# Image-wise window attention inside the merged plan, and layer 3 experts in three groups, in a four-layer kernel on one Trainium2 core

## The chip, the cores and the metric

The kernel runs on one core of one Trainium2 chip. The metric is device time in microseconds of one execution. A core has five engines with queues of their own, which wait for each other through semaphores: PE (matrix products into PSUM), DVE (vector work), ACT (activation functions), POOL (here it mostly issues indirect DMAs) and SP (issues plain DMAs). Each engine takes its instructions strictly in the order in which they were written into its queue.

## The reference, cut to what matters

The input is two images of 256 channels and 32 x 32 positions, all in fp32. Four layers follow each other. Layers 0 and 1 are attention over image positions and are not touched. Then the images become tokens `t` (two images of 1024 tokens of width 256), and layers 2 and 3 follow:

```
t = t + window_attention(layernorm(t))      # layer 2: 8 heads of 32, windows of 64 tokens, relative bias, shifted by 32
t = t + experts2(layernorm(t))              # 8 experts, hidden 1024, each token goes to its best 2, weights renormalised
t = t + additive_attention(layernorm(t))    # layer 3: e[i,j] = Wa . tanh(q[i] + k[j] + bh), softmax over the 1024 keys
t = t + experts3(layernorm(t))              # 8 experts, hidden 512, each token goes to its best 2
x = tokens back to channels
```

The window attention's softmax runs inside a window of 64 tokens, so an image's result depends on that image alone, as do the additive attention and the experts. In the last window of an image some pairs are masked.

## The kernel before, in words

Tokens lie in `t`, 16 tiles of 128 (8 for each image). Up to and with layer 1 a scheduler of the framework, or an order written out in `attention` and `shared_attention`, sets the instructions' order; both kernels have the same instructions there. After that come two parts.

*Window attention* (`window_attention`, L682 to 808). All 16 tiles are normalised (`layer_norm`, L89), turned to channels (`to_channels`, L103), and then treated tile by tile in one function with pools of its own: `project` makes queries and keys for four tiles at once (products L727, evictions of 32 partitions x 512 by turns on ACT L735 and DVE L737), `scores` makes values and scores (L747, L759), the scale and bias (L764), maximum and subtraction (L768, L769) and the exps (L772), and `values` turns the weights (L777), copies them (L779 on ACT, L780 on DVE), multiplies (L783), divides, turns, and applies the output matrix (L796). POOL adds the result to `t` (L801). Products use a PSUM pool of two buffers, the scores one of two, the turned weights one of their own, the values two. The framework's scheduler orders all of it. When the last tile of image 0 is through, `after` puts the whole of image 0's `dispatch` for layer 2 into the stream, so it runs beside the window attention of image 1.

*The merged plan* (`Late.run`, L1391). Everything else is a list of generators. Each generator's body stops at `yield` after a piece of work. The list gives each a start, an end and a number of pieces on a scale of its own; a heap takes the generator that is due next, lets it issue one piece, and puts it back by (end - start) / pieces. This writes out a fixed order for every engine (`manual_schedule`); no piece moves by itself at run time, and a piece whose inputs are late holds up what stands behind it on the same engine.

The generators, for layer `l` and image `b`:

- `dispatch(l, b)`: normalises 8 tiles in two halves (`normed`), finds each token's two experts and its slot (`route`, some 60 small DVE operations, products L1023 and L1055), in layer 2 normalises again, and writes the tokens into `slots_in[b]` in DRAM by 16 indirect DMAs on POOL (L989), two for each tile. Last it adds the second bias (L998 to L1004).
- `experts(l, b)`: 23 slot tiles of 128 slots (16 full ones and 7 for the experts' remainders). For each: two indirect DMAs on POOL fetch the expert's weights (L1140, three buffers each), SP loads the slots (L1150), PE turns them (L1158), up products (L1183), bias on DVE (L1188), gelu on ACT (L1172), down products (L1197), a copy on DVE (L1201), and SP stores the tile to `slots_out[b]`.
- `collect(l, b)`: 16 indirect gathers on POOL (L1241, eight buffers), weighted sums into `t` (L1254); in layer 2 then the norm and the projections for the additive attention (`project`, L1294), in layer 3 the way back to channels (`finish`, L1271) and the output.
- `additive(b)`: 64 steps, each four tanhs of 128 x 1024 on ACT (L1322, eight buffers) and eight products with a narrow picking matrix (L1331); after some of the tiles a batch of softmax exps (L1349), and then a turn (L1361) and a values product (L1368) for each tile, one a step.

PSUM of the plan: `misc`, two buffers for all small products, one for `ps_x`, two for `ps_h`, one for `ps_y`, and two banks for `ps_e` of the additive attention.

The order of the plan is: experts of layer 2, image 0, with image 1's dispatch; collect 0 and the start of image 1's experts; these with additive attention of image 0; collect 1; additive attention of image 1 with dispatch, experts and collect of layer 3 of image 0; and then dispatch, experts and collect of layer 3 of image 1, with nothing beside them.

## Time and profile before

| what | us |
|---|---|
| median of three runs (lowest, highest) | 3222.25 (3217.42, 3225.37) |
| the profiled execution's own time | 3233.88 |
| its span, first to last instruction | 3232.2 |
| PE busy (share of the span) | 2927.0 (91%) |
| DVE busy | 1886.4 (58%) |
| ACT busy | 2000.8 (62%) |
| POOL busy | 390.9 (12%) |

One execution is profiled; its time is given beside its span, since sums over the profile are sums over that execution. A PE that counts as busy isn't always at its peak: products overlap, and their ends are modelled. The profile counts an fp32 product with 128 or more columns as two records. A line of the kernel can be that of a helper that many parts call, so groups are told apart by the tiles they write. "Idle before" tells what ended the wait of an engine; it costs something only where that engine is what the end waits for. The last instruction of layer 1 is at about 1790 us in the span; the window attention ends at 2022, and the plan takes the rest.

### The profile page before, as it was taken

How to read it: one execution, taken by the hardware profiler on the slowest of the kernel's cores; microseconds unless marked ns; L12 is line 12 of the kernel's file. 1: busy time of each engine (PE TensorE's matmuls, PEld its weight loads, DVE VectorE, ACT ScalarE, POOL GpSimd, SP SyncE). 2: the span in 40 equal slices, each digit the busy share in tenths (PEclk: the TensorE clock that was granted, in tenths of full speed). 3: DMA queues.
4: the chain of work that ended last, by engine and by line, in shares of the span. 5: the costliest groups of instructions: out<-in, count | busy, mean ns of one | idle time of the engine just before them, and what ended most of it. 6: DMA issues, size and time to landing. Idle time of an engine off the chain costs nothing. (4 is left out here: it accounts for less than half of the span.)

```text
span 3232.2 us, 71102 instructions
## 1 busy us (share of the span) xinstructions
PE 2927.0 (91%) x29260; PEld 1890.0 (58%) x29260; DVE 1886.4 (58%) x3668; ACT 2000.8 (62%) x2990; POOL 390.9 (12%) x544
## 2 busy tenths in 40 slices
PE   7999999999999998999999788888699988999565
PEld 4566666666666665566676565776566633564355
DVE  5998898989898986354454574532422243222423
ACT  1887887878788875565566231111399878979200
POOL 3000000000000000000000002232311011322043
PEclk9999999999999998999999887899799998999688
DMA  3000000000000001000000100765554310543066
GB/s 119 3 3 3 3 3 3 3 3 3 3 3 3 3 3 28 1 1 1 1 2 2 24 1 27 269 232 205 208 182 172 134 30 19 175 147 95 19 229 198
DMA packets 175859, 206.85 MB, mean 64 GB/s; under 512 B 118368, under 2 KB 144880, under 8 KB 163760
## 3 DMA queue, kind: packets, MB, share of 16 engines
q0 software_dynamic: 34848, 167.82, 14.8%
q1 hardware_dynamic: 139248, 34.04, 4.8%
q8 instruction: 230, 3.77, 0.5%
q14 instruction: 93, 0.76, 0.1%
q10 hardware_dynamic: 1440, 0.47, 0.1%
HBM read 172.97 MB, written 28.57 MB: 62 GB/s over the span
## 5 line engine op out<-in xcount | busy, mean ns | idle before, releaser
L314 ACT ACTIVATE sc<-sc,sa_shift 128x1024 f32<-128x1024 f32 x512 | 585.1, 1148 | 53.5 <-DMA sa_shift<-sa_min 53.4
L1322 ACT ACTIVATE th<-kT,qb 128x1024 f32<-128x1024 f32 x512 | 541.0, 1134 | 73.7 <-PE ps_e L1331 58.3
L277 PE MATMUL ps_s<-kT,qT 64*32 64x512 f32 x8192 | 504.4, 596 | 9.0 <-ACT sc L287 8.7
L353 PE MATMUL ps_o<-wt,v 128*64 128x128 f32 x6144 | 503.4, 276 | 0.0
L353 PEld LDWEIGHTS ps_o<-wt,v 128*64 128x64 f32 x6144 | 442.2, 137 | 42.6 <-issue 42.6
L327 DVE STREAM_TRANSPOSE wt<-sc 128x768 f32<-128x768 f32 x512 | 465.7, 943 | 1.0 <-ACT sc L314 1.0
L287 ACT COPY sc<-ps_s 128x1024 f32<-128x1024 f32 x256 | 257.4, 1006 | 115.9 <-PE ps_s L277 42.7
L1172 ACT ACTIVATE h<-hb 128x512 f32<-128x512 f32 x138 | 86.1, 624 | 388.0 <-DVE hb L1188 333.8
L1183 PEld LDWEIGHTS ps_h<-xe,ew 128*128 128x128 f32 x2208 | 275.3, 201 | 79.3 <-issue 56.6
L1183 PE MATMUL ps_h<-xe,ew 128*128 128x128 f32 x2208 | 289.9, 288 | 30.4 <-DMA ew<-in_l_up,rt_rows 28.0
L298 DVE TENSOR_REDUCE sa_least<-sc 128x1 f32<-128x1024 f32 x256 | 306.1, 1196 | 1.9 <-ACT sc L287 1.9
L284 DVE TENSOR_SCALAR_CACHE_REDUCE sc<-ps_s 128x1024 f32<-128x1024 f32 x256 | 301.3, 1177 | 5.9 <-PE ps_s L277 5.9
L1331 PE MATMUL ps_e<-th,pick 128*32 128x512 f32 x2048 | 295.2, 616 | 1.4 <-DVE sc_a L1338 1.4
L1197 PE MATMUL ps_y<-ew,h 128*128 128x256 f32 x1104 | 260.6, 386 | 3.9 <-ACT h L1172 2.7
L1188 DVE TENSOR_TENSOR hb<-ps_h,ew 128x512 f32<-128x512 f32 x138 | 95.3, 691 | 280.8 <-PE ps_h L1183 239.2
L154 DVE TENSOR_SCALAR_CACHE_REDUCE sc<-ps_s 128x1024 f32<-128x1024 f32 x128 | 151.8, 1223 | 179.3 <-PE ps_s L148 179.3
L353 PE MATMUL ps_o<-wl,v_odd 128*64 128x128 f32 x2048 | 252.1, 277 | 0.0
L277 PEld LDWEIGHTS ps_s<-kT,qT 64*32 64x32 f32 x8192 | 126.9, 106 | 200.8 <-issue 171.4
L1197 PEld LDWEIGHTS ps_y<-ew,h 128*128 128x128 f32 x1104 | 204.5, 192 | 59.8 <-issue 20.5
L335 PEld LDWEIGHTS ps_t<-ident,sc 128*128 128x128 f32 x1024 | 107.5, 141 | 216.1 <-issue 169.1
L353 PEld LDWEIGHTS ps_o<-wl,v_odd 128*64 128x64 f32 x2048 | 221.3, 137 | 0.0
L335 PE MATMUL ps_t<-ident,sc 128*128 128x128 f32 x1024 | 168.5, 287 | 4.8 <-ACT wl L336 4.1
(269 smaller groups left out, 3607.1 us busy)
## 6 DMA issues: line engine op xcount, KB each, us to landing
xr<-slots_in SPq DMA_DIRECT2D x92, 128.0 KB
slots_out<-y SPq DMA_DIRECT2D x92, 128.0 KB
sa_got<-sa_least SPq DMA_DIRECT2D x512, 0.5 KB
sa_shift<-sa_min SPq DMA_DIRECT2D x512, 0.2 KB
slots_in<-zero POOLq DMA_DIRECT2D x46, 128.0 KB
sa_sums<-sa_total SPq DMA_DIRECT2D x256, 1.0 KB
xT<-in_x SPq DMA_DIRECT2D x4, 496.0 KB
sb_l_w_in<-in_l_w_in SPq DMA_DIRECT2D x1, 1536.0 KB
```

The costliest lines, as they stand in the source:

```text
L277: nc.tensor.matmul(ps[r][S * c : S * (c + 1), a, :].rearrange("p (b i) -> p b i", i=S), lhsT=qT[half, p, S * i : S * (i + 1)], rhs=keys[ha ...
L284: nc.vector.tensor_scalar(scores[m][0], flat[0], 1.0, None, ALU.mult, ALU.min, accum_out=least[m // 2][:, 0, h : h + 1])
L287: nc.scalar.copy(scores[m][1], flat[1])
L298: nc.vector.tensor_reduce(least[m // 2][:, 1, h : h + 1], scores[m][1], AX.X, ALU.min)
L314: nc.scalar.activation(scores[m][r], scores[m][r], AF.Exp, bias=shift[m // 2][:, r : r + 1], scale=-1.0, accum_out=total[i][:, 2 * p + r, ...
L327: nc.vector.transpose(weights[i, h][:, 2 * p + r, :], scores[m][r][:, :DIRECT])
L335: nc.tensor.transpose(ps[:, g, r, :], s[:, at : at + P], self.ident)
L353: nc.tensor.matmul(sums[i][64 * k : 64 * (k + 1)], lhsT=values, rhs=w, start=(h == 0 and j == 0 and t == 0), stop=(h == 1 and j == 1 and t ...
L1183: nc.tensor.matmul(ps[:, j, :], lhsT=a[:, c, at : at + P], rhs=x[:, c, :], start=(c == 0), stop=(c == CC - 1),)
L1197: nc.tensor.matmul(ps, lhsT=h[:, j, :], rhs=w2[:, j, :], start=(j == 0), stop=(j == HB - 1))
L1322: nc.scalar.activation(h, keys, AF.Tanh, bias=self.qb[b][:, s // G, g : g + 1])
L1331: nc.tensor.matmul(pe[i][c * U : (c + 1) * U, a, :], lhsT=self.pick[:, k, :], rhs=h[:, a, :], start=(k == 0), stop=(k == G - 1),)
```

## The change

- The norm over all tiles, its way to channels and `window_attention` go. `windows(b)` does one image as a generator of the plan, with 128 columns a projection instead of 512, and a fixed order: in step `i` the scores and weights of tile `i`, the turn of tile `i - 1`, the projection of `i + 1`, the back-turn of `i - 2`, the values of `i - 1` and the output of `i - 3`. All its products but scores and values use the plan's two `misc` buffers.
- The plan has names, and each entry tells which others must have been issued before it. Image 0's windows are alone at the start (W0); then come image 0's dispatch (D20) and experts (E20) with image 1's windows (W1) and its dispatch (D21).
- Layer 3's experts are in three groups: image 0 (16 slot tiles and 7), and the two halves of image 1 (8 and 7, that is 15 slot tiles each). The first half's dispatch may start when the additive attention has issued half of image 1; its experts lie beside the second half. The second half alone comes after it.
- Pools: window and additive parts share SBUF and PSUM in phases (`open`); the gather has five buffers and runs two tiles ahead (eight and four before); the additive scores have three buffers (four); softmax batches end after tiles 3, 6, 8 for image 0 and 2, 4, 6, 7, 8 for image 1 (before: 4, 7, 8 for both).

```diff
+GROUPS = {
+    (2, 0): range(0, IT), (2, 1): range(IT, NT),
+    (3, 0): range(0, IT), (3, 1): range(IT, IT + IT // 2), (3, 2): range(IT + IT // 2, NT),
+}
+SLOT_TILES = {IT: 2 * N // TILE + E - 1, IT // 2: N // TILE + E - 1}
...
-            late = Late(ctx, self, t)
-            with tc.tile_pool(name="tok2", bufs=1) as tok2:
...
-                self.window_attention(t, u, uT, after)
-            late.run()
+            Late(ctx, self, t).run()
...
-    def dispatch(self, l, b):
+    def dispatch(self, *key):
...
-        for half in range(2):
-            yield from self.normed(b, half)
-        yield from self.route(l, b)
+        for half in range(n // 4):
+            yield from self.normed(key, tokens, half)
+        yield from self.route(key, n)
...
-                y = self.sb.tile([P, C], F32, name="got", bufs=8)
+                y = self.moe.tile([P, C], F32, name="got", bufs=5)
...
-        for i in range(4):
+        for i in range(2):
             gather(i)
-        yield
+            yield
...
+    def windows(self, b):
+        nc, t, H, D = self.nc, self.t, 8, 32
+        tokens, key = GROUPS[2, b], ("w", b)
+        for half in range(2):
+            yield from self.normed(key, tokens, half)
...
+        def project(g):
+            q[g] = sb.tile([D, H, P], F32, name="qh")
+            k[g] = sb.tile([D, H, P], F32, name="kh")
+            for o in range(2 * CC):
+                ps = self.misc([P, P], "ps_qk")
+                for c in range(CC):
+                    nc.tensor.matmul(
+                        ps, lhsT=self.w_qkv[:, c, o * P : (o + 1) * P], rhs=uT[:, c, g * P : (g + 1) * P],
+                        start=(c == 0), stop=(c == CC - 1),
+                    )
+                for r in range(4):
+                    to = (q if o < CC else k)[g][:, (o % CC) * 4 + r, :]
+                    rows = slice(D * r, D * (r + 1))
+                    if r % 2:
+                        nc.scalar.activation(to, ps[rows, :], AF.Identity, bias=self.b_qk[rows, o : o + 1])
+                    else:
+                        nc.vector.tensor_scalar(to, ps[rows, :], self.b_qk[rows, o : o + 1], None, ALU.add)
+                yield
...
+        yield from project(0)
+        for i in range(IT + 3):
+            if i < IT:
+                scores(i)
+                weigh(i)
+            yield
+            if 0 < i <= IT:
+                turn(i - 1)
+            yield
+            if i + 1 < IT:
+                yield from project(i + 1)
+            if 1 < i <= IT + 1:
+                back(i - 2)
+            yield
+            if 0 < i <= IT:
+                values(i - 1)
+            if 2 < i:
+                output(i - 3)
+            yield
...
-        batches = {3: range(4), 6: range(4, 7), 7: range(7, 8)}
+        ends = (3, 6, 8) if b == 0 else (2, 4, 6, 7, 8)
+        batches = {e - 1: range(d, e) for d, e in zip((0, *ends), ends)}
...
-            (self.experts(2, 0), 0, 185, 72),
-            (self.dispatch(2, 1), 5, 165, 48),
-            (self.collect(2, 0), 186, 225, 18),
-            (self.experts(2, 1), 186, 480, 72),
-            (self.additive(0), 226, 535, 65),
-            (self.collect(2, 1), 482, 525, 18),
-            (self.additive(1), 536, 850, 65),
-            (self.dispatch(3, 0), 546, 622, 40),
-            (self.experts(3, 0), 625, 790, 50),
-            (self.collect(3, 0), 795, 840, 11),
-            (self.dispatch(3, 1), 880, 900, 40),
-            (self.experts(3, 1), 905, 1000, 50),
-            (self.collect(3, 1), 1001, 1040, 11),
+            "W0": (self.windows(0), (), -110, 0, 74),
+            "W1": (self.windows(1), ("W0",), 1, 175, 74),
+            "D20": (self.dispatch(2, 0), ("W0",), 1, 60, 48),
+            "E20": (self.experts(2, 0), ("D20",), 62, 280, 72),
+            "D21": (self.dispatch(2, 1), ("W1",), 176, 272, 48),
+            "C20": (self.collect(2, 0), ("E20", "W1"), 281, 325, 20),
+            "E21": (self.experts(2, 1), ("D21",), 281, 600, 72),
+            "A0": (self.additive(0), ("C20",), 326, 640, 65),
+            "C21": (self.collect(2, 1), ("E21",), 601, 642, 20),
+            "A1": (self.additive(1), ("C21", "A0"), 643, 960, 65),
+            "D30": (self.dispatch(3, 0), ("A0",), 655, 710, 36),
+            "E30": (self.experts(3, 0), ("D30",), 715, 850, 50),
+            "C30": (self.collect(3, 0), ("E30",), 855, 890, 13),
+            "D31": (self.dispatch(3, 1), ("A1 half",), 830, 870, 24),
+            "E31": (self.experts(3, 1), ("D31",), 880, 965, 34),
+            "C31": (self.collect(3, 1), ("E31",), 1030, 1050, 8),
+            "D32": (self.dispatch(3, 2), ("A1",), 970, 1000, 24),
+            "E32": (self.experts(3, 2), ("D32",), 1001, 1060, 34),
+            "C32": (self.collect(3, 2), ("E32",), 1061, 1080, 8),
```

## The prediction

> **What bounds the kernel now.** I read the slices of the page first (the TensorE clock falls and PE has gaps only after 1790 us), then the busy time by stage. I cut the stages at the starts and ends of lines L1183 (up), L1322 (tanh) and L1241 (gather) in the timeline.
>
> ```profile
> 1815.00:2022.00 207.00, 171.32 (x1193) 127.52 (x1191) 120.51 (x333) 58.06 (x98) 29.50 (x45) 0.79 0.03 11
> 2029.00:2259.00 230.00, 197.34 (x1222) 176.54 (x1222) 92.29 (x278) 33.11 (x50) 55.00 (x57) 0.93 0.65 237
> 2278.00:2595.00 317.00, 305.29 (x2094) 204.74 (x2097) 91.50 (x212) 252.74 (x267) 46.67 (x50) 0.97 0.47 170
> 2595.00:2672.00 77.00, 59.59 (x313) 24.36 (x312) 34.13 (x99) 53.83 (x54) 15.32 (x16) 0.91 0.10 29
> 2672.00:3004.00 332.00, 312.51 (x1900) 163.24 (x1904) 97.13 (x264) 294.49 (x300) 74.75 (x78) 0.94 0.33 107
> 3004.00:3100.00 96.00, 34.23 (x116) 21.67 (x109) 33.35 (x135) 2.78 (x4) 21.34 (x22) 0.57 0.14 47
> 3100.00:3199.00 99.00, 90.27 (x594) 81.42 (x592) 33.38 (x67) 14.49 (x23) 37.87 (x40) 0.99 0.84 283
> 3199.00:3232.20 33.20, 5.58 (x17) 2.95 (x16) 10.74 (x21) 0.00 (x0) 15.30 (x16) 0.58 0.34 99
> ```
>
> Columns: stretch, length, busy PE, weight loads, DVE, ACT, POOL (us), clock, DMA share, GB/s. The rows are: window attention of both images, with image 0's dispatch in its middle; layer 2 experts of image 0; experts of image 1 beside additive attention of image 0; the collect between; additive attention of image 1 beside layer 3 experts of image 0; then, with nothing beside it, image 1's layer 3 dispatch, experts and collect. Rows 3 and 5 have little idle PE. The last three, 228 us, run alone; the sixth is a latency chain. Its cause stands in the chain of waits: each scatter waits for the one before.
>
> ```profile
> 3068.78 2.40 DMA slots_in<-u,rt_slot
> 3071.45 2.41 DMA slots_in<-u,rt_slot
> 3074.12 2.42 DMA slots_in<-u,rt_slot
> ```
>
> They start 2.67 us apart; 16 take 42.7 us, and the experts' weight fetches stand behind them on POOL.
>
> The third view is the timeline of ACT and DVE in the window attention:
>
> ```profile
> 1858.65 0.68 ACT L735 ACTIVATE qh<-ps_mm,sb_b_qk 32x512 f32<-32x512 f32 x1 [4.30 <-DVE qh L737]
> 1860.14 1.45 ACT L735 ACTIVATE qh<-ps_mm,sb_b_qk 32x512 f32<-32x512 f32 x2 [0.81 <-DVE qh L737]
> 1859.36 1.52 DVE L737 TENSOR_SCALAR qh<-ps_mm,sb_b_qk 32x512 f32<-32x512 f32 x2 [0.75 <-ACT qh L735]
> ```
>
> The four evictions of one product go by turns: while one engine reads that PSUM tile the other waits.
>
> [...]
>
> **The change, part by part** (against the profiled execution: span 3232.2, own time 3233.9, which is 11.6 over the median of 3222.25). I set new times of the same events against the old ones.
>
> *Image 0's attention alone.* Norms and the first evictions come at 1816 (1815 now; the query weights still load first). Then one tile after another, in the order written. From its scores: DVE scale, max, subtract 3 x 0.69 = 2.1; ACT two exps 1.3 and a copy of turned weights 0.6, by 4.1. All products share two PSUM buffers, so the next tile's projection starts only when that copy frees one: product and hand-over 0.7, then sixteen evictions of 32x128. They are not in the trace; 32x512 takes 0.74 and 0.68, [...] 0.35 is my value (0.27 to 0.40, from a 128x128 ACT copy at 0.27 and a DVE step of that size at 0.40). By turns, three slots a product, they end 5.1 later at 9.8. Transposes, values, output, v and scores then go over PE and the freed buffers, 3 to 3.5. A tile takes 13 us (11 to 14). First tiles 1816 to 1842.5, five at 13, drain 17.5: 1925. (Now: some 43 us for four tiles, 10.7 each, ordered by the scheduler.)
>
> *Image 0's dispatch, with image 1's attention begun.* DVE does both: 59 us of listed operations (four half norms at 7.4, from 4 x (0.40 + 0.18 + 0.41) + 12 x 0.165 + 2 x 0.69; the second norm 8, routing 14, two softmax tiles and projections 7), 6 for gaps of 0.03 between 190 small ones, 9 waiting for PE transposes, router and turns. The first scatter comes at 2000. Fifteen more steps of 2.67 give 2040; image 0's weight fetches are queued behind them, at 2042; fetch to first up product was 6.5 (2022.4 to 2028.9): 2048, against 2029 now. Now the scatters (1943 to 1995) hide behind image 1's attention; in the new order only two and a half of its tiles are there to cover them. Cost 19.
>
> *Image 0's experts with the rest of image 1's attention.* A dense tile is 7.2 us (y copies, L1201, at 2233.15, 2240.39, 2247.64) and that is PE. A window tile is 7.4 us of PE: 32 records at 0.11, 8 at 0.216, 32 score records at 0.03, ten transposes at 0.11. Some 7 of 8 are left, 51 us, over 14 expert tiles: 14 x 7.2 + 51/0.95 + 0.8 a tile for in-order waits and table loads = 166. On POOL every window tile puts a memset and an add (0.7 to 1.0) between weight fetches, and the add waits for DVE; I cost that at nothing, because fetches run two to three tiles, over 20 us, ahead. Without that cover it would be about 1 us for each of eight tiles. Nine tiles are left, 65, with image 1's dispatch, 10, and late fetches, 10: 85. The end is 2299 against 2259: +40. (Now the scatters stretch six tiles to 10 to 16 us each; that loss of 37 goes, since the scatters stand behind nearly all fetches. It is in the 85.)
>
> *Collect 0.* Twelve gathers stand ahead of image 1's first fetch, where it was eight or nine: +4 at 0.96 each. Experts begin at 2322, +44. The stretch up to image 1's first tanh keeps its 394 us: three more tanh steps lie beside the experts (+6) and three fewer beside the collect.
>
> *Additive attention of image 1.* It has 64 steps of four tanhs. Layer 3 experts of image 0 stand after step 12 in the new order (19 in the old). Their dispatch, which begins with the stage, takes 34 us to its first scatter (as 3016 to 3049.5 now), 43 of scatters and 8 to the first product: +85, some 15 us after PE comes to them. PE waits in order, and ACT, two steps of buffers ahead, soon after. Then 28 steps x 1.72 + 23 tiles x 3.73 + 4 values jobs x 4.3 = 151 of PE, /0.96 = 157 (now 172 for 37 steps). Six steps at 4.6 and the dispatch's products: 34. Then the added fifteen tiles: 56, with 16.5 steps 28 and three jobs 13, /0.96 = 101; 8 for their scatters behind collect's gathers. Together 385 (365 to 405) against 332: +53. Splitting the last image makes 30 tiles of 23, and the first 15 are paid here, since PE was already 312 of 332 busy.
>
> *Tail.* Now 228. The half group needs one norm half less and smaller routing: first scatter at +36 (45.5 now), eight scatters 21.4, +8 to the first product: +65. Fifteen tiles at 4.25 and the second group's collect beside them, eight gathers on POOL and four more stores on SP among the loads: 70 (99 now). Four token tiles to collect: 23 (33 now). 158: -70.
>
> Sum: 44 + 53 - 70 = +27; 3222.25 + 27 is about **3249**. Two more exp batches in image 1 cost 2 x 2 x 1.28 = 5 on ACT, behind PE there. Smaller gather buffers cost nothing while three us pass from issue to use (five buffers at 0.96). Bounds: the front 44 (15 to 75), additive stage 53 (30 to 75), tail -70 (-62 to -80).
>
> **Rivals.** *Faster, the added tiles are free.* The place is the additive stage of image 1: were its PE records long only because PE waits inside, fifteen tiles would ride on ACT's 294 of 332 us. For it: the clock is 0.94 and the tanhs pace that stage. Against it: experts beside it run 6 to 12 us a tile where alone they take 4.2. Growth 10 instead of 53: 27 - 43 = -16, 3206; it decides once the growth is under 16. With the front at its low bound of 15 as well, 3177. *Same:* window tiles at the present 10.7 (eight save 18) and the dispatch 10 quicker: 27 - 28, 3221. *Slower still:* window products in image 0's experts stop PE at the two shared buffers: 2 us in each of 14 tiles, 28, and a second dispatch late by 17: 27 + 45, 3294.
>
> **How the numbers follow.** About 0.3% (10 us) is what a measurement of this kernel can tell from none. Main case, slower by 10 to 50: 0.50; slower still: 0.13; the same: 0.13; faster: 0.24. Range 3188 to 3300; the main case alone 3232 to 3272.
>
> **What would show it.** Right: image 0's first up product at 2035 to 2060; scores of image 0 some 13 us apart; image 1's tanhs over 370 us; 155 us from the last tanh to the end. Wrong: tanhs of image 1 within 345 us, or the first experts ending before 2265; either gives the faster case.

## The result and the profile after

The changed kernel takes 3353.07 us (median of four; 3350.96 to 3362.24) beside 3223.4 for the kernel before on the same chip: ratio 1.0411, 95% interval 1.0387 to 1.0435. On another chip it took 3354.4 beside 3241.3: 1.0357 (1.0335 to 1.0379). So it is slower by 113 to 130; the kernel before differs more from chip to chip than the changed one. The profiled executions have spans of 3349.7 and 3232.2 us, 117.5 apart, and all stage times below are theirs.

| event, us in the span | before | forecast | changed |
|---|---|---|---|
| image 0's windows added to `t`, last tile | 1912.7 | 1925 | 1950.5 |
| first scatter, layer 2 image 0 | 1943.1 | 2000 | 2014.5 |
| first up product, image 0 | 2028.9 | 2048 | 2077.2 |
| last expert tile, image 0 | 2259.3 | 2299 | 2332.6 |
| first up product, image 1 | 2278.0 | 2322 | 2373.8 |
| first tanh of image 1 | 2672.3 | 2716 | 2754.3 |
| last tanh | 3003.7 | 3101 | 3186.6 |
| end of the span | 3232.2 | 3259 | 3349.7 |

Up to image 1's first tanh the loss is 82 (44 forecast), in its additive stage 101 (53), and behind it there is a gain of 65 (70). The busy time by stage of the changed kernel, with the columns of the prediction's first fence:

```profile
1810.80:1950.50 139.70, 118.53 (x651) 96.80 (x649) 55.85 (x131) 40.66 (x96) 6.09 (x14) 0.57 0.00 1
1950.50:2077.20 126.70, 60.45 (x276) 43.68 (x276) 70.09 (x263) 11.99 (x30) 21.69 (x26) 0.52 0.16 60
2077.20:2332.60 255.40, 231.76 (x1680) 214.41 (x1678) 130.60 (x363) 74.64 (x127) 55.08 (x64) 0.95 0.55 198
2332.60:2373.80 41.20, 15.52 (x41) 7.56 (x42) 16.80 (x54) 0.00 (x0) 22.60 (x23) 0.59 0.48 163
2373.80:2754.30 380.50, 358.55 (x2386) 224.62 (x2385) 115.90 (x278) 308.83 (x323) 57.12 (x60) 0.96 0.39 139
2754.30:2848.00 93.70, 73.79 (x315) 27.39 (x313) 35.17 (x137) 58.98 (x57) 21.27 (x22) 0.75 0.15 53
2848.00:3020.30 172.30, 163.51 (x1130) 112.71 (x1130) 54.65 (x140) 134.96 (x142) 37.75 (x40) 0.97 0.49 159
3020.30:3077.40 57.10, 35.54 (x176) 11.40 (x169) 19.22 (x67) 35.25 (x34) 29.36 (x30) 0.64 0.37 117
3077.40:3186.60 109.20, 104.30 (x722) 70.84 (x720) 30.47 (x65) 85.18 (x90) 22.65 (x24) 0.98 0.49 160
3186.60:3349.70 163.10, 89.13 (x483) 73.19 (x480) 54.15 (x162) 13.40 (x20) 51.56 (x54) 0.75 0.44 147
```

In order: image 0's windows alone; its dispatch; its experts; the collect; experts of image 1 with additive attention of image 0; then image 1's additive stage in four pieces (ahead of, during and behind image 0's layer 3 experts, and with the half group's); the tail. In the first row PE is busy for 118.5 of 139.7 us, and yet its clock is 0.57. In row 4 POOL and DMA work while PE waits. Rows 6 and 8 are stretches of the additive stage in which both PE and ACT have idle time.

The timeline of PE in one tile of image 0's windows shows what the first row is made of (start, duration in us, engine, line, operation, count):

```profile
1870.19 0.69 PE L1237 MATMUL ps_o<-ident,o 128*128 128x128 f32 x2 [0.29 <-ACT kh L1176]
1870.67 3.46 PE L1226 MATMUL ps_av<-va,w_ptT 128*128 128x33 f32 x16
1873.94 2.05 PE L1245 MATMUL ps_wo<-sb_wa_w_out,oT 128*128 128x256 f32 x4
1875.79 1.91 PE L1186 MATMUL ps_va<-sb_w_qkv,uT 128*128 128x256 f32 x4
1877.63 1.97 PE L1198 MATMUL ps_s<-kh,qh 32*64 32x64 f32 x32
```

There is no gap between these; the sixteen values records take 0.22 us each. (They are eight products: in these traces an fp32 product of 33, 64 or 8 columns counts as two records too, and only a turn as one.) In the kernel before, where the clock went up and down within the window stage (0.79 on average), eight such records took 1.05 us in a stretch at clock 1.00 (1848.7 to 1849.8), where eight take 1.73 here at 0.50:

```profile
1848.71 1.05 PE L783 MATMUL ps_av<-va,ptT 128*128 128x33 f32 x8 [0.53 <-ACT ptT L779]
```

The changed kernel's steady tiles are 17.3 us apart (the scaled scores, L1205, at 1897.1, 1914.4 and 1931.6), where 13 were forecast. PE's waits over four such tiles, 1862 to 1932 (us in total, how many, the longest):

```profile
PE ps_qk L1168 <- DVE w_ptT L1221: 5.5, 4, 1.8
PE ps_qk L1168 <- ACT qh L1176: 1.2, 4, 0.3
PE ps_o L1237 <- ACT kh L1176: 1.2, 4, 0.3
```

That is 8 us in 70: PE is hardly kept waiting, it is slow. The next three fences are lines of POOL's timeline: at the end of image 0's layer 2 experts in the changed kernel, the first gather at that place in the kernel before, and ahead of the first half group's experts in the changed kernel (gathers between the lines shown are left out):

```profile
2343.58 0.97 POOL L827 DMA_INDIRECT slots_in<-u,rt_slot  x1 [1.70 <-DMA slots_in<-u,rt_slot]
2344.85 0.98 POOL L1082 DMA_INDIRECT got<-slots_out,rt_slot  x1 [0.30 <-issue]
```

```profile
2261.94 0.96 POOL L1241 DMA_INDIRECT got<-slots_out,rt_slot  x1 [20.37 <-issue]
```

```profile
3056.13 1.08 POOL L1082 DMA_INDIRECT got<-slots_out,rt_slot  x1 [1.02 <-DVE t L1095]
3064.01 1.08 POOL L1082 DMA_INDIRECT got<-slots_out,rt_slot  x1 [5.54 <-DVE t L1095]
3067.96 0.95 POOL L979 DMA_INDIRECT ew<-in_l_up,rt_rows  x1 [0.30 <-issue]
```

Image 0's last expert tile was out at 2332.6, but its gathers stand behind image 1's late scatters until 2344.9, 12.3 us later; in the kernel before it was 2.6 (2259.3 to 2261.9). And the half group's first weight fetch stands behind image 0's sixteen gathers, which themselves wait for the sums that free their five buffers.

### The profile page after: what moved, and what is told of

Its sections match the earlier page's. It is cut to its first block, busy times and chain, and to the rows that moved or that the text cites. A ratio compares the mean times of both kernels' runs of the same rounds, so it can differ in the third digit from the quotient of the medians.

```text
span 3349.7 us, 72263 instructions
## 1 busy us (share of the span) xinstructions
PE 2994.4 (89%) x29638; PEld 1966.7 (59%) x29638; DVE 1947.5 (58%) x3892; ACT 2051.0 (61%) x3107; POOL 402.5 (12%) x558
## 5 line engine op out<-in xcount | busy, mean ns | idle before, releaser
L1022 PEld LDWEIGHTS ps_h<-xe,ew 128*128 128x128 f32 x2320 | 282.2, 197 | 61.5 <-issue 42.4
L1022 PE MATMUL ps_h<-xe,ew 128*128 128x128 f32 x2320 | 297.0, 283 | 11.6 <-DMA ew<-in_l_up,rt_rows 4.7
L1036 PE MATMUL ps_y<-ew,h 128*128 128x256 f32 x1160 | 277.7, 389 | 15.8 <-DMA ew<-in_l_down,rt_rows 9.2
L1324 PE MATMUL ps_e<-th,pick 128*32 128x512 f32 x2048 | 283.7, 633 | 5.4 <-DVE sc_a L1331 5.4
L1036 PEld LDWEIGHTS ps_y<-ew,h 128*128 128x128 f32 x1160 | 217.1, 194 | 81.6 <-issue 33.5
L1040 DVE COPY y<-ps_y 128x256 f32<-128x256 f32 x99 | 42.0, 424 | 242.7 <-PE ps_y L1036 242.5
```

Of the source, the lines that this page charges most:

```text
L1022: nc.tensor.matmul(ps[:, j, :], lhsT=a[:, c, at : at + P], rhs=x[:, c, :], start=(c == 0), stop=(c == CC - 1),)
L1036: nc.tensor.matmul(ps, lhsT=h[:, j, :], rhs=w2[:, j, :], start=(j == 0), stop=(j == HB - 1))
L1324: nc.tensor.matmul(pe[i][c * U : (c + 1) * U, a, :], lhsT=self.pick[:, k, :], rhs=h[:, a, :], start=(k == 0), stop=(k == G - 1),)
```

## The experiments

The series ran on different chips, each beside the kernel before. Ratios are to that one; spans and events are those of the profiled executions (L1 ends at 1787 to 1792 in all of them). W0 is the last of image 0's windows, U the first up product of image 0, C the gap between the experts of image 0 and image 1 in layer 2, T image 1's first tanh, A its additive stage, tail the rest. In the changed kernel's variants that leave a stage and its plan alone, W0 lies between 1947.6 and 1952.4 and A between 432 and 437, whatever the series, so larger differences in these two columns are the edits'.

| run | W0 | U | C | T | A | tail | span | ratio (95%) |
|---|---|---|---|---|---|---|---|---|
| before | 1912.7 | 2028.9 | 19 | 2672 | 331 | 228 | 3232.2 | 1 |
| changed | 1950.5 | 2077.2 | 41 | 2754 | 432 | 163 | 3349.7 | 1.0411 (1.0387-1.0435) |
| e15, the same again | 1947.6 | 2075.0 | 41 | 2752 | 433 | 165 | 3350.0 | 1.0357 (1.0335-1.0379) |
| e1 groups only | 1930.4 | 2046.9 | 11 | 2687 | 439 | 165 | 3291.4 | 1.0160 (1.0138-1.0181) |
| e2 windows only | 1952.4 | 2079.6 | 41 | 2760 | 340 | 234 | 3334.0 | 1.0294 (1.0271-1.0316) |
| e3 project by four | 1928.3 | 2050.0 | 31 | 2718 | 433 | 163 | 3314.9 | 1.0262 (1.0239-1.0284) |
| e4 wide spare products | 1918.8 | 2046.5 | 41 | 2729 | 433 | 168 | 3330.3 | 1.0271 (1.0250-1.0292) |
| e18 narrow spare products | 2033.1 | 2158.7 | 41 | 2841 | 434 | 159 | 3433.9 | 1.0618 (1.0585-1.0651) |
| e5 collect late | 1948.4 | 2075.9 | 41 | 2756 | 420 | 167 | 3342.2 | 1.0310 (1.0292-1.0327) |
| e6 experts late | 1949.2 | 2076.3 | 39 | 2753 | 417 | 163 | 3333.6 | 1.0321 (1.0304-1.0338) |
| e9 layer 3 retimed | 1948.3 | 2075.8 | 41 | 2759 | 392 | 162 | 3313.7 | 1.0222 (1.0197-1.0246) |
| e7 windows early | 1949.1 | 2101.2 | 9 | 2770 | 437 | 163 | 3370.1 | 1.0430 (1.0413-1.0448) |
| e13 windows denser | 1948.8 | 2066.9 | 8 | 2770 | 437 | 166 | 3373.2 | 1.0411 (1.0388-1.0434) |
| e14 three mended | 1921.5 | 2041.0 | 7 | 2736 | 394 | 162 | 3291.3 | 1.0174 (1.0152-1.0195) |
| e10 all but e13 | 1919.6 | 2046.6 | 31 | 2718 | 389 | 164 | 3272.0 | 1.0121 (1.0098-1.0144) |
| e8 groups, retimed | 1928.4 | 2044.5 | 11 | 2682 | 419 | 161 | 3260.9 | 1.0078 (1.0051-1.0104) |
| e11 groups, retimed further | 1914.9 | 2032.3 | 11 | 2676 | 407 | 161 | 3243.8 | 1.0031 (1.0018-1.0044) |
| e17 with a spared tail | 1917.0 | 2035.1 | 11 | 2675 | 413 | 163 | 3250.5 | 1.0039 (1.0021-1.0058) |
| e12 before, spare products | 1919.2 | 2046.1 | 19 | 2697 | 326 | 228 | 3250.9 | 1.0037 (1.0023-1.0052) |
| e16 before, spared tail | 1920.0 | 2036.3 | 18 | 2688 | 330 | 231 | 3249.0 | 1.0008 (0.9997-1.0019) |

The front of e16 is that of the kernel before, instruction for instruction, and its first tanh comes at 2688: differences of up to 16 between series in that column are the chips'.

### One half of the change alone (e1, e2)

e1 keeps the old window attention, e2 the old two groups:

```diff
-        self.phase, self.issued = None, set()
-        self.open("windows")
+        self.phase, self.issued = None, {"W0", "W1", "D20"}
+        self.open("attention")
```

```diff
-    (3, 0): range(0, IT), (3, 1): range(IT, IT + IT // 2), (3, 2): range(IT + IT // 2, NT),
+    (3, 0): range(0, IT), (3, 1): range(IT, NT),
```

> Window attention as in the kernel before (both images ahead of the plan, image 0's dispatch inside it), with only the second half of the change: layer 3 in three groups, the gather's five buffers, the softmax batches, the new plan from image 1's additive attention on. Theory (the loss is the sum of two nearly independent parts, as the stage times of the changed kernel's profile give them: +82 up to image 1's first tanh from the windows, +100 from there to its last tanh and -64 after it from the groups): about 3223 + 36 = 3259, first tanh at 2672 +- 10, additive stage 425 to 440, tail 160 to 165. Rival (the additive stage is long because the windows' pools and late collects disturb it): additive stage under 400, total at or under 3225.

> The windows in the plan as in the changed kernel, but layer 3 in two groups with the plan times of the kernel before (shifted to the new scale). Theory (two nearly independent parts): 3223 + 82 = 3305, first tanh of image 1 at 2754 +- 10, additive stage about 335, tail about 228. Rival (the windows are nearly free and the groups cost the most): at or under 3260.

The additive stage stays at 439 without the new windows and the front at 2760 without the new groups, so neither disturbs the other. From the first tanh to the end e1 takes 604 us against 560 before, +44; the windows put the first tanh 72 to 87 later. Both lose, the windows nearly twice as much. The ratios don't split so cleanly: 1.6% and 2.9% are more than the whole, and e1's first tanh, 2687, and its span, 3291, are over the 2662 to 2682 and the 3259 expected. Beside the groups, e1 and e8 alter one thing more: the old windows' output tile `y` has one buffer for two. Their W0 is 1930 and 1928, where e11 and e17, with two buffers, have 1915 and 1917. So the groups' own loss is the 44, and not all of the 1.6%. e2's span, 3334, is over the 3305 expected; its stages are within 10 of theirs.

### What a window tile waits for (e3, e4, e18)

e3 makes queries and keys for four tiles at once, as before. e4 and e18 put spare products, whose results nobody reads, ahead of each query and key product of image 0:

```diff
-                ps = self.misc([P, P], "ps_qk")
+                ps = self.misc([P, CH], "ps_qk")
...
-                            ps, lhsT=self.w_qkv[:, c, o * P : (o + 1) * P], rhs=uT[:, c, g * P : (g + 1) * P],
+                            ps, lhsT=self.w_qkv[:, c, o * P : (o + 1) * P], rhs=uT[:, c, g * CH : (g + 1) * CH],
```

```diff
+                if b == 0:
+                    spare = self.p_y.tile([P, C], F32, name="ps_y")
+                    for _ in range(2):
+                        nc.tensor.matmul(spare, lhsT=self.w_qkv[:, 0, 0:P], rhs=self.w_qkv[:, 1, 0:C], start=True, stop=True)
```

> The changed kernel, but the windows project queries and keys for four tiles at once (512 columns, 32x512 evictions) as the kernel before did, so 32 products and 128 small evictions of an image become 8 and 32. Theory (the sixteen small evictions of a tile by turns, 5.5 of its 16.1 us, are serial with the rest): image 0's windows alone take about 8 x 5.5 - 2 x 8 = 28 less, 113 instead of 141; total about 3353 - 28 - 5 = 3320. Rival (PE at half clock is what sets the pace of a tile, 120 of 141 us are PE busy at 0.57): image 0's windows shorten by under 12, total over 3338.

> The changed kernel with two products of 128x256 more ahead of each query and key product of image 0's windows, into a PSUM bank that is free then; nobody reads them, so no wait is added or taken away. PE gets 64 products more. Theory (PE runs at half clock in image 0's windows, 0.57, because it pauses, and its own products after the evictions then take 6.5 us a tile where 3.5 were expected): the clock there rises over 0.8 and the windows get shorter by 10 to 25, total 3330 to 3345. Rival (the waits on evictions and buffers set the pace, the low clock is only their mark): the windows get longer by 0 to 40, the clock rises all the same.

e3 took 22 off the windows (28 expected). Its query and key products have 512 columns, and its clock there is 0.66 for 0.57, so the 22 can't be put down to the evictions alone. e4 took 32 off: PE did 64 products more in 32 us less. Its busy time, and its timeline over the same piece of a tile:

```profile
1809.00:1918.80 109.80, 96.47 (x782) 82.29 (x781) 56.40 (x133) 40.79 (x96) 6.08 (x14) 0.96 0.00 1
```

```profile
1857.43 1.87 PE L1230 MATMUL ps_av<-va,w_ptT 128*128 128x33 f32 x16
1859.14 1.11 PE L1249 MATMUL ps_wo<-sb_wa_w_out,oT 128*128 128x256 f32 x4
1860.09 1.03 PE L1190 MATMUL ps_va<-sb_w_qkv,uT 128*128 128x256 f32 x4
1861.04 1.15 PE L1202 MATMUL ps_s<-kh,qh 32*64 32x64 f32 x32
```

Every product takes little more than half as long as in the changed kernel (1.87 for 3.46), and a steady tile takes 12.8 us. PE's waits over four tiles fall only from 8 us to 5, a small part of the 18 that these tiles got shorter. Two readings were left: the spare products fill PE's pauses, or they are wide. e18 uses nine of 128x32 in place of two of 128x256:

> As the run with spare products in image 0's windows, but the spare products are narrow: nine of 128x32 ahead of each query and key product instead of two of 128x256, about the same PE time (18 records at 0.11 or a little less at half clock, against 4 at 0.26 at full clock). Read by nobody. Theory (the clock follows how much the products stream, not whether PE has something to do; the windows' own products of 33 and 64 columns ran 10.8 us without a gap at 0.50): the clock stays under 0.65, and image 0's windows last 145 to 185 us. Rival (any work that fills PE's pauses lifts the clock): clock over 0.9 and windows of 105 to 122 us, as with the wide ones.

```profile
1809.00:1950.50 141.50, 141.50 (x779) 136.40 (x779) 34.86 (x82) 25.20 (x60) 0.89 (x3) 0.52 0.00 1
```

```profile
1893.18 3.89 PE L1169 MATMUL ps_y<-sb_w_qkv 128*128 128x32 f32 x18
1898.30 3.46 PE L1230 MATMUL ps_av<-va,w_ptT 128*128 128x33 f32 x16
```

PE is busy for all of these 141.5 us, with no pause, and its clock is 0.52; the values records take 3.46 us as in the changed kernel. The windows last to 2033 (222 us from 1811, longer than the 185 expected): eighteen of the 32-column records take 3.89 us, 0.21 each, where 0.11 was assumed. So to fill the pauses was not enough here. PE, fed mostly with products of 32 columns, stayed at 0.52 though it was full; four records of 256 columns in each round lifted it to 0.96.

The changed kernel itself points the same way. Its widest products are those of 256 columns (L1245, L1186), next to each other once in a tile. In each of the three tiles behind the one shown, the clock was 1.00, 0.98 and 0.99 over some 3 us just after them (1896.5 to 1899.7, 1914 to 1917 and 1931 to 1934), and the turns that fell into it took 1.09 us, where those of the tile shown, at 0.50, took 1.97:

```profile
1896.99 1.09 PE L1220 MATMUL ps_wpt<-ident,probs 128*128 128x128 f32 x8
```

Products of 128 columns are not narrow in this sense: in e16 (below) two bursts of them ran at 1.00 (3029.7 to 3033.8 and 3036.5 to 3041), and a third, right behind routing products at 0.50, at 0.82 on average (3051.6 to 3059.6). No run separates what counts in a wide product, its columns or the fewer weight loads beside them, nor how much the changed kernel's own pauses (21 of 140 us) add.

### The additive stage: places in the plan (e5, e6, e9)

```diff
-            "E30": (self.experts(3, 0), ("D30",), 715, 850, 50),
-            "C30": (self.collect(3, 0), ("E30",), 855, 890, 13),
+            "E30": (self.experts(3, 0), ("D30",), 745, 872, 50),
+            "C30": (self.collect(3, 0), ("E30",), 905, 945, 13),
```

e5 has the second line alone, e6 the first; e9 has both, and the dispatches D30 at 665 to 733 and D31 at 818 to 866.

> The changed kernel, with one pair of numbers altered: layer 3's collect of image 0 is due at 905 to 945 instead of 855 to 890, so its sixteen gathers no longer stand ahead of the first half group's weight fetches on POOL. Theory (those gathers, 35 us long, hold the fetches, and so the 57 us from the last product of image 0's experts to the first of the next group, where 34 were predicted): that gap falls to 30 to 40, image 1's additive stage from 432 to 408 to 418, total 15 to 25 less than the changed kernel. Rival (the gap is the half group's own dispatch and six additive steps): gap over 50, total within 6.

> The changed kernel, with layer 3's experts of image 0 due at 745 to 872 instead of 715 to 850, so that they stand behind some 19 additive steps on PE instead of 13. Theory (their first product waits for the scatters in any case, and PE and ACT, in order, idle behind it): the first product stays at 90 to 96 us after image 1's first tanh, 18 to 20 steps are done by then instead of 13, and the additive stage and the total fall by 12 to 25. Rival (PE has no free time in the stage taken as a whole, so steps put before the experts are only moved): total within 6 of the changed kernel.

> The changed kernel with the plan times of layer 3 alone altered: experts of image 0 at 745 to 872 and collect at 905 to 945 as tried apart, and both dispatches slower in the plan (665 to 733 and 818 to 866), so that their products for routing stand behind more additive steps on PE. Theory (the additive stage's growth over the forecast is PE waiting in order, behind scatters, behind DVE's routing chain, and the fetches behind the gathers): the additive stage falls from 432 to 385 to 402, the total by 30 to 45. Rival (PE's own work of the added tiles): stage over 410.

e5: the gap ahead of the half group's experts falls from 57 to 38, the stage by 12, to 420 (408 to 418 expected), and the span by 7.5 (15 to 25); a few us come back, since the gathers now lie among those experts' fetches (112 us for 107). e6: the stage falls by 15, but not as expected. The first product came 115 us after the first tanh instead of 94, with 19 steps of products ahead of it instead of 13. The experts then took 158 for 172, and the gap behind them 36 for 57. e9: 392, 40 less than the changed kernel and 7 over the forecast; its span is 36 less. The same pieces as above, in e9:

```profile
2759.00:2863.50 104.50, 92.90 (x442) 34.50 (x441) 39.50 (x146) 85.89 (x85) 21.25 (x22) 0.87 0.15 55
2863.50:3018.50 155.00, 151.60 (x1080) 104.14 (x1082) 56.39 (x167) 126.14 (x133) 43.28 (x46) 1.00 0.54 177
3018.50:3034.10 15.60, 12.89 (x80) 3.58 (x72) 3.47 (x10) 13.70 (x14) 8.08 (x9) 0.89 0.56 189
3034.10:3149.20 115.10, 107.22 (x726) 74.32 (x726) 39.14 (x83) 83.43 (x89) 38.63 (x40) 0.96 0.55 178
```

The second row is now full of PE work at clock 1.00, and the gap is 15.6. What the changed kernel had in its place is seen in PE's timeline at the start of its stage:

```profile
2766.82 2.21 PE L792 MATMUL ps_tr<-ident,u 128*128 128x128 f32 x8 [5.63 <-DVE u L781]
2774.87 2.21 PE L792 MATMUL ps_tr<-ident,u 128*128 128x128 f32 x8 [3.39 <-DVE u L781]
2777.01 7.00 PE L861 MATMUL ps_router<-sb_gate_w,uT 128*128 128x8 f32 x32
```

PE stands before each turn until DVE has normalised, and then gives 7 us to the routing products; ACT, two steps of buffers ahead, issues four tanhs at 2772 and the next only at 2788. (Additive products lie between the lines shown.)

### The front: where image 1's windows and scatters lie (e7, e13)

```diff
-            "W1": (self.windows(1), ("W0",), 1, 175, 74),
+            "W1": (self.windows(1), ("W0",), 1, 100, 74),
...
-            "D21": (self.dispatch(2, 1), ("W1",), 176, 272, 48),
+            "D21": (self.dispatch(2, 1), ("W1",), 101, 200, 48),
```

e13 has 30, 150 and 151, 245 in these places.

> The changed kernel, with image 1's windows due at 1 to 100 instead of 1 to 175 and image 1's layer 2 dispatch at 101 to 200 instead of 176 to 272. Theory (the dispatch of image 0 leaves PE at half empty for over 110 us, where only two and a half window tiles lie, and the late dispatch of image 1 holds the collect's gathers): the second scatters end over 40 us before the experts do, the gap between the experts of image 0 and image 1 falls from 41 to about 23, two window tiles leave the experts' stretch (-15), and DVE's turns for them put the first scatter back by 10; image 1's first tanh comes 15 to 30 earlier. Rival (DVE's order in the dispatch decides: what the windows gain the first scatter loses): first tanh within 8 of 2754.

> The changed kernel with image 1's windows due at 30 to 150 (1 to 175) and its layer 2 dispatch at 151 to 245 (176 to 272): later than the run in which they began early, but denser, so that the dispatch comes some five expert tiles sooner. Theory (two separate losses in the front after the windows: image 1's window tiles between the dispatch's DVE steps, and the late scatters of image 1 that hold the collect's gathers on POOL): first scatter 5 to 10 sooner than in the changed kernel, the gap between the experts of image 0 and image 1 down from 41 to about 25, image 1's first tanh 15 to 25 sooner. Rival (the window tiles cost the same wherever they lie, and the gap is gathers, sums and projections in any case): first tanh within 8.

Both closed the gap (9 and 8 us) and both lost: the first tanh came 15 to 16 later, where each theory had it sooner and each rival within 8. In e7 the first scatter came 13 later and the first product 24 later, by the mechanism of its rival. In e13 the first product came 10 sooner, as expected, but the experts then took 299 us instead of 255. More of the sixteen scatters that wait for one another (1.7 to 7.1 us at a time between 2262 and 2330) now lie among the weight fetches on POOL. e13's busy time over the later part of its experts, and PE's longest waits in all of them (us in total, how many, the longest):

```profile
2200.00:2280.00 80.00, 66.80 (x398) 60.96 (x399) 49.80 (x184) 11.51 (x17) 13.53 (x14) 0.85 0.48 173
2280.00:2365.70 85.70, 62.07 (x311) 51.04 (x309) 18.06 (x43) 7.06 (x12) 27.05 (x28) 0.80 0.58 215
```

```profile
PE ps_h L1022 <- DMA ew<-in_l_up,rt_rows: 16.4, 2, 10.9
```

PE is idle for 43 of 299 us (24 of 255 in the changed kernel), 37 of them in these two rows, and what it does there runs at 0.80 to 0.85. That scatters among the fetches are the cause is argued, not shown: e7's lie there too (2237 to 2299), and its experts took 262.

A shorter gap also gains less than it seems. In all runs with a gap of 31 us or more, the stretch from image 1's first up product to its first tanh lasts 379 to 384 us; in all with a gap of 19 or less, 394 to 400. So about half of what the gap loses is work that only moves across its end.

### Together (e10, e14), and the remedies on the other kernels (e8, e11, e12, e16, e17)

e14 is e4 with the places of e13 and e9. e10 is e3 with the places of e9 and 92 wide spare products in image 0's windows, 11 or 12 a tile.

> The changed kernel with all three found costs mended: the spare products in image 0's windows (clock), image 1's windows at 30 to 150 with its dispatch at 151 to 245, and the new plan times of layer 3. Theory (they are separate, so they add up: -32, -15 to -25 and -36 of the changed kernel's span): span 3255 to 3270, 1.008 to 1.013 of the kernel before; what is left over the forecast of +27 is then under 15. Rival (they meet in the same wait): over 3280.

> The changed kernel with the new layer 3 times, projections for four tiles at once and spare products in image 0's windows (about 14 of 128x256 a tile, into a free PSUM bank, read by nobody). Theory (clock and small evictions both cost in image 0's windows, and the two gains add up to most of it): image 0's windows 141 -> 85 to 100, image 1's first tanh at 2700 to 2715, total 3265 to 3285. Rival (the gains share one cause, the wait at each tile's end): windows over 108, as in the runs with one of both.

e14 misses its theory because e13's part was a loss and no gain. Beside e13 it has the first tanh 34 sooner (e4 gained 25 there) and the stage 43 shorter (e9's times: 40), so those two don't meet in one wait. e10 has the windows no shorter than e4, against its theory. PE was busy for 84 of the first 89 us at clock 1.00, so the spare products were perhaps too many; no run had fewer. It is the quickest with the new windows: 78 of the 117.5 us are gone, and its first product (2046.6), first tanh (2718) and stage (389) stand within 5 of the forecast's 2048, 2716 and 385.

e8 and e11 are e1 with layer 3 retimed as in e5 and e6 (e8), and as in e9 (e11, which also has the two buffers for `y` of the kernel before). e17 is e11 with the half group's collect at 882 to 894 beside the last dispatch, and spare products in that dispatch. e12 is the kernel before with 128 spare products of 256 columns in its windows, in a bank taken from the scores, which keep one buffer; e16 is the kernel before with spare products of 128 columns in its last dispatch alone (20 ahead of each half's turn, 30 ahead of the counts, 100 behind the second bias).

> The kernel with the old window attention and the new groups (first series), with both retimings of layer 3: image 0's experts 30 later on the plan's scale, image 0's collect 50 later. Theory (the additive stage of 439 us there holds two idle stretches that are the plan's, not the work's): the stage falls to 395 to 415, the whole by 25 to 40, to 1.003 to 1.008 of the kernel before. Rival (PE is full with the added tiles): over 1.012 of the kernel before.

> The old window attention, with its pools nearer to the kernel before than in the first series, and the three groups with the new layer 3 times. Theory (windows are the larger loss; the groups, once nothing stands idle behind a dispatch, give back in the additive stage what they save at the end): first tanh of image 1 at 2670 to 2685, additive stage 390 to 405, tail 160, total 0.997 to 1.003 of the kernel before. Rival (the added tiles' PE work is not hidden): additive stage over 412, total over 1.006.

> The old windows with the three groups and the retimed layer 3, and two things more: spare products in the last half group's dispatch as in the run beside it (60 at its end), and the first half group's collect beside that dispatch instead of beside the last experts. Theory (both shorten the tail of 167 us: -5 from the clock, -8 from gathers that no longer stand among the last fetches): tail 150 to 158, total 0.998 to 1.002 of the kernel before. Rival (the gathers and sums only move into the dispatch's own chain): tail over 162.

> The kernel before, with spare products of 128x256 in its window attention (eight for each group projection and six a tile, 112 in all, into a bank taken from the scores, which have one buffer instead of two; read by nobody). Theory (a PE that pauses is slowed, also there: 0.79 over its 207 us): clock over 0.9 and the window stage 10 to 30 shorter, total 0.992 to 0.997 of the kernel before. Rival (there the pauses are DVE's and ACT's, and PE's own time isn't on the path): within 0.2%, or longer by the spare products' time.

> The kernel before with spare products of 128x128 in the last dispatch only (20 ahead of each half's turn to channels, 30 ahead of the counts, 100 behind the second bias while the scatters run), in the bank of the down products, which is free then; read by nobody. Nothing waits for it. Theory (PE at 0.57 there serves a chain: turns, router and counts, some 14 us of PE at half clock, and the first expert tiles): dispatch and first tile 6 to 10 shorter, total 0.997 to 0.999 of the kernel before. Rival (the chain is DVE and scatters, PE's share is small or the spare products stand in its way): within 0.1%, or slower.

e8 gave 30 back (its stage, 419, is 4 over the range expected) and e11 17 more, some 5 of them ahead of the first tanh: 1.0031, still above 1. e11's additive stage is 407, over the 390 to 405 expected; the tail saves 68 and the stage pays 76. e17's tail is 163, as its rival had it, where 150 to 158 were expected; its two edits weren't tried apart. e12 lifted the clock of the window stage from 0.79 to 0.91, and lost 0.4%: PE was busy for 171 of 207 us there before, and in its first 110 us for 109.5 with the spare products. (No wait of PE on the scores' single buffer shows.) e16 changed nothing that can be measured. The stretches of e16 over a spare burst and over the routing products behind it, and then the kernel before over its routing products (columns as in the first fence):

```profile
3036.50:3041.00 4.50, 4.50 (x42) 4.39 (x40) 4.12 (x17) 0.00 (x0) 0.00 (x0) 1.00 0.01 2
3044.60:3051.60 7.00, 6.99 (x33) 6.99 (x33) 0.55 (x1) 0.00 (x0) 0.00 (x0) 0.50 0.00 0
```

```profile
3031.30:3038.30 7.00, 7.00 (x33) 6.90 (x32) 0.69 (x1) 0.00 (x0) 0.00 (x0) 0.50 0.00 0
```

The burst, 40 records of 128 columns, ran at 1.00. Its end and the routing products are 3.6 us apart, with eight turns and 1.9 us of waits between; the 32 records of 8 columns are at 0.50 again and take the same 7.00 us. No version tried beats the kernel before.

### The changed kernel again (e15)

Unaltered, as the reference on the chip of e13 and e14.

> The changed kernel unaltered, beside the other two on their chip, as their reference: 1.038 to 1.044 of the kernel before, span 3345 to 3360. If it came under 1.035, part of the differences between series would be the chips'.

1.0357 lies below the interval of the first chip and below the 1.038 to 1.044 expected, while the changed kernel's own time is the same (3354.4): the difference is the kernel before's. Ratios of different series are uncertain by some 0.5%, and the readings above therefore rest on stages.

## Why the prediction was wrong, step by step

The direction and the three mechanisms were right: the front and the additive stage grow, the tail shrinks. Two sums were too small by 38 and 47, and the tail's gain was too large by 5. Two steps failed: PE's rate in image 0's windows (25 of the 38), and in the additive stage the assumption that PE runs through the work of each piece without standing (the 47).

- *Image 0's attention alone, 13 us a tile.* The step that failed is "Transposes, values, output, v and scores then go over PE and the freed buffers, 3 to 3.5." They take 8.7 to 9.4 us in the trace (3.46, 2.05, 1.91 and 1.97 for the last four). The evictions were right (0.34 and 0.36 for 0.35; 5.6 us a tile for 5.1). The mis-sized term is PE's rate: I priced records as they are at clock 1.00, and these ran at 0.50. With the clock lifted to 0.96 (e4) the tile is 12.8 and the windows end at 1919, against 13 and 1925 forecast. That 12.8 meets 13 is in part luck: at clock 1.00 these products still take 5.0 (1857.2 to 1862.1 in e4), near what the prediction's own record prices add up to (18 at 0.11, 8 at 0.216, 32 at 0.03: 4.7), and what made up for it is that the next projection starts 2.8 us after the scores, not 4.1. The windows are 25 of the 38 (1950.5 for 1925).
- *The reason for a slow PE.* I took the clocks of 0.57 and 0.79 in the kernel before for the mark of PE's pauses, as the theories of e4 and e12 do; that was my assumption, which no trace had shown. In the runs 10.8 us of products without a gap ran at 0.50 (the changed kernel, from 1870.2), and 141.5 us without a gap at 0.52 (e18): there it was not pauses that kept the clock down. For the 0.57 of the last dispatch, where PE is busy for 34 of 96 us, no run shows the cause.
- *The turns of the evictions.* Right as a forecast: in the changed kernel ACT stands 0.17 to 0.41 us before each eviction of a tile until DVE's is done (L1176 behind L1178, 1866 to 1871). What asks for these turns, and what it would bring to drop them, no run shows.
- *Image 0's dispatch.* 64 us to the first scatter for 75; 46.5 of scatters for 40; from the last to the first product 16 for 8, because a window tile's products (7.2 us at 0.50, 2070.1 to 2077.2) were written ahead of it. Together +4.
- *Image 0's experts with image 1's windows.* 255 for 251. The sum is right by luck: the first 14 tiles took 156 (166 forecast), the other nine 100 (85).
- *Collect 0, +4, and the stretch up to image 1's first tanh.* The gap was +22, and the stretch 380 for 394. Together they are 422 for 417, since part of the work moves across the boundary (above), so the sum of the front is only 5 out here. The late second dispatch stood in the prediction as part of the rival "slower still", with 17; that its scatters come last on POOL was foreseen, that image 0's gathers stand behind them was not in the main sum. The other part of that rival, PE stopping at the two shared buffers beside the experts, didn't come.
- *Additive stage.* First product +94 (85 forecast), experts 172 (157), the piece behind them 57 (34), the half group's experts up to the last tanh 109 (101 and 8 for gathers). I counted the work in each piece and let PE run through it at 0.96. In the order as written PE stands behind DVE at the dispatches' turns (5.6 and 3.4 at once in the fence above), and POOL has sixteen gathers ahead of the half group's fetches. e9 takes 40 of the 47 away by times in the plan alone, and reaches 392 for the 385 forecast; its pieces are not the forecast's, though (105, 155, 16 and 117 us).
- *The added tiles.* "Splitting the last image makes 30 tiles of 23, and the first 15 are paid here" holds: even retimed, e11's stage is 76 longer than before.
- *Tail.* 163 for 158.
- *Rivals.* "Faster, the added tiles are free" falls with e9 and e11. "Slower still" was half right, and too small.

Not settled: what a better place of image 1's scatters could bring in the front (e7 and e13 found none).

## What to carry to other kernels

Before pricing products from another stage, look at the clock that the new stage will have: here PE was full for 141.5 us and still ran at 0.52, mostly on records of 32 columns (e18). When work is moved into a fixed order, walk each queue past it; here forty us of the loss came from gathers, routing products and experts standing ahead of work that was ready, and a few numbers in the plan took them out. And compare events, not gaps: a gap that closes can move its work into the next stretch. Splitting a group to shorten a tail pays for the padding of each part where the split part now runs.

## What the runs showed of the hardware

- In image 0's windows the granted clock followed the width of the products, not only PE's pauses: 0.52 with PE 100% busy for 141.5 us, mostly on records of 32 columns (e18); 0.96 with four records of 256 columns ahead of each projection product (e4), which made 141.5 us of work into 109.8 with 64 products more. A burst of 40 records of 128 columns ran at 1.00, one of 60 behind routing products at 0.82 on average (e16).
- 32 routing records of 8 columns took 7.00 us at 0.50 without a pause, 3.6 us after such a burst at 1.00 (with eight turns and 1.9 us of waits between, e16).
- An eviction of 32x128 from PSUM took 0.34 us on DVE and 0.36 on ACT, one of 32x512 0.74 and 0.68: a quarter of the size for half the time.
- A table load on ACT took 1283 ns (L1172 and L1349 of the kernel before), the 1.28 of the prediction.
- PE's busy share doesn't tell whether spare products pay. They took 32 us off a stage with PE 85% busy at clock 0.57 (e4), and added 0.4% to the kernel before, where the stage was 83% busy at 0.79 (e12).
